# The start of a graph layer: one node tile first, more node tables, and another pace of getting ahead

## The chip, the cores and the metric

The kernel runs on one core of a Trainium2 chip. The metric is the time of one execution on the device, in microseconds; lower is better. The engines named here are TensorE (PE, matrix products; PEld is its weight load), VectorE (DVE), ScalarE (ACT), GpSimd (POOL) and SyncE (SP), which issues most DMAs. Each engine takes its own list of instructions, and semaphores order the lists against each other.

## The reference, cut to what matters

```python
def ssp(x): return softplus(x) - log(2)

h0  = relu(layernorm(x))                                  # x: 12500 nodes x 128
h   = h0 @ W_in2f
Wij = ssp(edge_attr_20 @ W_f1 + b_f1) @ W_f2 + b_f2       # 412500 edges, 20 -> 128 -> 128
Wij = Wij * edge_weight[:, None]
x_ij = h[dst] * Wij                                       # one row of h for each edge
agg = segment_sum(x_ij, src, 12500)                       # summed by the other end
out = x + ssp(agg @ W_o1 + b_o1) @ W_o2 + b_o2
```

The edges are sorted by `dst`, so a run of neighbouring edges needs a few neighbouring rows of `h`. `src` is in no order.

## The kernel before, in words

The edges are cut into 806 chunks of 512 (four tiles of 128). For a chunk the kernel makes an edge value `v` (128 x 512) and a picked node row `hg`, multiplies them into `o` and scatters the rows of `o` by `src` into slot tables in DRAM. Later the slots of a node are loaded back, added and put through the output layer. The steps of a chunk, with the lines of the kernel before:

- `hidden` (L668): two products with `wf1` give `z` for a pair of chunks. `hidden_log` (L675 to L677): ScalarE's Abs, Exp and Ln. `hidden_end` (L684): VectorE makes `r`.
- `value` (L769, L771): four products with `wf2` into the PSUM tile `v` and a fifth, `ones_b` by `bf12_p`, that adds the bias. The bias stands in `bf12_p` as three bfloat16 parts, which `biases` (L306 to L309) and `bias_parts` (L316 to L320) make once.
- `rows` (L621, L623): SyncE reads the chunk's place in the node table from `shifts` and loads 32 rows of the table `h3_t[t]` (`near`). `window` (L760): `at` marks which of these rows an edge wants. `pick` (L780): products of `at` and `near`. `picked` (L789): ScalarE scales by the edge weight into `hg`.
- `columns` (L630 to L658): for 8 groups of 16 tiles, VectorE splits `src` into block and place. `blocks` (L689): `inb`. `rank` and `rank_end` (L708, L741, L713, L733 to L737): two products on the running count `free`, its maximum `top` and the slot number of each edge.
- `message` (L798, L800, L804): VectorE makes `o` from `v` and `hg`; GpSimd issues four indirect DMAs of 128 rows.

The node rows `h` are made by the generator `make_h`, one quad (four tiles of 128 nodes) at a time: load, statistics (L343, L344), a scale `rs` by Ln and Exp on ScalarE (L347, L348), normalisation (L352 to L359), transposes (L364), Relu (L366), product with `win` (L370), and three bfloat16 parts of the result (L372 to L378). It stores them to `h3` and to each small table that holds some of these nodes (L384, L393). A chunk reads from one table alone, `table_of[c]`, so it needn't wait for later quads: table 0 holds the first quad and serves 9 chunks; table q + 1 holds quad q and some tiles on either side. The transposes, the product of `make_h` and the bias product `b12` (L308) all use PSUM tiles of one tag, `acc`, which has one buffer.

The order on every engine is the order in which the program makes the instructions (`tc.manual_schedule()`). A prologue makes constants, the first quad and the first chunk's parts. Then a loop calls `step(k)` for each chunk: message of chunk k, then parts of later chunks, so far ahead as bounds in `step` say. Steps with `k < 10` are not `steady` and their leads grow: the window, the pick and the count (`rank`, up to `k + LR`, LR = 6). After each step the generators in `h` and, later, those of `side` (further quads and the rest of the index work) go on by one yield. DMAs from SyncE and ScalarE share eight semaphores in turn, so that an issue waits until the DMA eight before it has landed.

Of the kernel before, what the change touches and what calls it, by code (L numbers as in the profile page):

```python
# [41 lines left out]
def gnn_kernel(  # L42
# [84 lines left out]


    tables = [(0, QN)]
# [4 lines left out]
    for c in range(NC):  # L134
        n = c * CH * N // n_edges
        table_of.append(0 if n < QN - NEAR - P else min(n // QN, NQ - 1) + 1)
# [46 lines left out]
    def load_x(q):  # L183
        n = min(QT, NTILE - q * QT)
        full = min(n, N // P - q * QT)
        xb = ln.tile([P, QT, P], F32, name="xb")
        if full < n:
            nc.vector.memset(xb[:, full:n, :], 0.0)
            nc.sync.dma_start(xb[:N % P, full, :], x[q * QN + full * P:N, :])
        if full:  # L190
            nc.sync.dma_start(xb[:, :full, :], x[q * QN:q * QN + full * P, :]
                              .rearrange("(c p) f -> p c f", p=P))
        return xb
# [60 lines left out]
    def constants():  # L254

        early[0] = load_x(0)
        part_load(0)
        first_load(0)
        nc.sync.dma_start(win, w_in2f)

        for j in range(NCHUNK):
            nc.sync.dma_start(wf1[32 * j:32 * j + RBF, :], w_f1)

        nc.scalar.preload_act_table_set("natural_log_exp_and_others")
        nc.scalar.dma_start(bf1, b_f1[:, None])
        nc.scalar.dma_start(wf2, w_f2)
        nc.scalar.dma_start(bf2, b_f2[None, :].to_broadcast([P, P]))
        make_identity(nc, ident)
        for _ in bounds(0, nc.gpsimd):
            pass  # L270

        prow_i = early_room[:WP, rows_at + 5 * NC:rows_at + 5 * NC + 1].bitcast(I32)
        nc.gpsimd.iota(prow_i, pattern=[[0, 1]], base=0, channel_multiplier=43)
        nc.gpsimd.iota(places, pattern=[[1, P]], base=0, channel_multiplier=0,
                       allow_small_or_imprecise_dtypes=True)

        nc.gpsimd.memset(after, 1.0)
        nc.gpsimd.affine_select(out=after, in_=after, compare_op=ALU.is_ge, fill=0.0, base=-1,
                                pattern=[[1, P]], channel_multiplier=-1)
        nc.gpsimd.memset(ones_b, 1.0)  # L280
        nc.gpsimd.memset(bf12_p, 0.0)
        nc.gpsimd.memset(zero, 0.0)

        nc.gpsimd.memset(before, 1.0)
        nc.gpsimd.affine_select(out=before, in_=before, compare_op=ALU.is_ge, fill=0.0, base=-1,
                                pattern=[[-1, P]], channel_multiplier=1)
        nc.gpsimd.iota(spare, pattern=[[1, 1]], base=N, channel_multiplier=1,
                       allow_small_or_imprecise_dtypes=True)
        nc.vector.memset(eps, EPS)
        nc.vector.memset(half, 0.5)  # L290
        nc.vector.memset(bad, 0.0)
        nc.vector.memset(rel[:, NPART - 1, :], 0.0)
        nc.vector.memset(ones, 1.0)
        nc.vector.memset(none, 0.0)

        for t in range(QT):
            nc.vector.memset(turn[:, :, t:t + 1], -1.0 if t % 2 else 1.0)
        nc.vector.tensor_scalar(prow_i, prow_i, 7, None, op0=ALU.logical_shift_right)
        nc.vector.tensor_copy(prow, prow_i)
        nc.vector.scalar_tensor_tensor(after, ident, BIG, after, op0=ALU.mult, op1=ALU.add)  # L300

        nc.vector.tensor_scalar(rest_of, after, -1.0, 1.0, op0=ALU.mult, op1=ALU.add)

    def biases(psum):

        nc.vector.tensor_scalar(nbf1, bf1, -1.0, None, op0=ALU.mult)  # L306
        b12 = psum.tile([P, QT, P], F32, name="b12", tag="acc")[:, 0, :]
        nc.tensor.matmul(b12, bf1.to_broadcast([P, P]), wf2, start=True, stop=True)  # L308
        nc.vector.tensor_add(bf12, b12, bf2)  # L309

    def bias_parts():

        left = bf12[:3, :]
        for k in range(3):
            part = ln.tile([3, P], BF16, name="bias_part", bufs=1)
            nc.vector.tensor_copy(part, left)  # L316
            nc.vector.scalar_tensor_tensor(bf12_p[:3, :], part, ident[:3, k:k + 1],
                                           bf12_p[:3, :], op0=ALU.mult, op1=ALU.add)
            if k < 2:
                nc.vector.tensor_sub(left, left, part)  # L320

    def late_loads():
        nc.sync.dma_start(wo1, w_o1)
        nc.sync.dma_start(wo2, w_o2)
        nc.sync.dma_start(bo1, b_o1[:, None])
        nc.sync.dma_start(bo2, b_o2[None, :].to_broadcast([P, P]))

    early = {}
    quads = []


    def make_h(q, psum):

        n = min(QT, NTILE - q * QT)
        xb = early.pop(q, None)
        if xb is None:
            xb = load_x(q)
            for _ in range(3):
                yield
# [39 lines left out]
        for (b, rows), table in zip(tables, h3_t):  # L379
            lo = max(0, b - q * QN) // P  # L380
            hi = min(n, (b + rows - q * QN) // P)
            if lo < hi:
                r = q * QN + lo * P - b
                nc.sync.dma_start(  # L384
                    table[r:r + (hi - lo) * P, :].rearrange("(c p) f -> p c f", p=P),
                    hb[:, lo:hi, :, :].rearrange("p c k f -> p c (k f)"))
                if b + rows == QN:
                    yield
            if q == NQ - 1:
                for r in range(NTILE * P - b, rows, P):  # L390
                    if r >= 0:
                        nc.sync.dma_start(table[r:r + P, :], none)
        nc.sync.dma_start(  # L393
            h3[q * QN:q * QN + n * P, :].rearrange("(c p) f -> p c f", p=P),
            hb[:, :n, :, :].rearrange("p c k f -> p c (k f)"))
        yield
# [136 lines left out]
    with tc.tile_pool(name="edge", bufs=2) as edge, tc.tile_pool(  # L533
# [45 lines left out]

        class Group:  # L580


            def __init__(self, g):
                self.g = g
                self.seg = next(s for s in segs if s.g0 * NCHUNK <= g * NCHUNK < s.c1)
                self.n = min(NCHUNK, NCH - g * NCHUNK)
                if g % NB == 0:
                    f = edge.tile([P, NB, CH], F32, name="f")
                    for j in range(NCHUNK):
                        nc.sync.dma_start(f[32 * j:32 * j + RBF, :, :],  # L590
# [3 lines left out]
                i = g - self.seg.g0  # L594
                if i % SB == 0:
                    w = min(SB, ceil_div(self.seg.c1, NCHUNK) - g) * TG
                    cols = slice(g * TG, g * TG + w)
                    src_i = edge.tile([P, SB * TG], I32, name="src_i")
                    nc.sync.dma_start(src_i[:, :w], src_t[:, cols])
# [5 lines left out]
                if g == 0:  # L605
                    rel_store(0)
                self.rel = edge.tile([WP, NCHUNK, CH], BF16, name="rel", bufs=4)
                nc.sync.dma_start(self.rel, rel_d[g * NCHUNK:(g + 1) * NCHUNK, :][None, :, :]
                                  .to_broadcast([WP, NCHUNK, CH]))
# [16 lines left out]
            def columns(self):  # L626
                if len(self.cols) == 3:
# [9 lines left out]
                    nc.vector.tensor_copy(place[:, :w], src_i[:, :w])  # L637

# [255 lines left out]
        NEXT = table_of.index(1) - 1  # L894
        LG, LW, LR, LZ = 12, 6, 6, 4

# [57 lines left out]
        def step(k, units=()):  # L954
# [6 lines left out]
            steady = k >= 10  # L961
            group((k + LG) // NCHUNK)
            part("rows", min(k + LW, 2 * k + 3, NEXT if k < NEXT - 3 else NCH), rows)
# [19 lines left out]
            if not steady:  # L983
                part("window", k + 1 if k < 1 else k + 2 if k < 6 else k + 3, window)
# [5 lines left out]
            part("pick", k + 1 if k < 8 else k + 2, pick)  # L990
# [10 lines left out]
            upto = max(made["rank"], min(k + LR, k + 1 + (k + 1) // 2))  # L1001
# [81 lines left out]
        def side():  # L1083

            others = rest()
            for i in range(1000):
                if i % 9 == 0 and 2 + i // 9 < NQ:
                    quads.append(make_h(2 + i // 9, psum))
# [3 lines left out]
                if i >= 5 and next(others, 1) and not quads and 2 + i // 9 >= NQ:  # L1092
                    return
                yield

        with tc.manual_schedule():
            constants()
            nc.scalar.activation(count_ps, places, AF.Copy)
            nc.scalar.activation(prow_ps, prow, AF.Copy)
            h = [make_h(q, psum) for q in range(2)]  # L1100
            next(h[0])
            next(h[0])
            relative(0)
            shift(0)
            group(0)
            early[1] = load_x(1)
            next(h[0])
            part("hidden", 0, hidden)
            part("blocks", 0, blocks)
            next(h[0])  # L1110
            ready = ranks(0)
            next(ready)
            next(h[0])
            part("log", 0, hidden_log)
            next(ready, None)
            made["rank"] = 0
            next(h[0])
            part("rows", 1, rows)
            biases(psum)
            part("end", 0, hidden_end)  # L1120
            part("window", 0, window)
            bias_parts()
            group(1)
            aside = side()
            for k in range(-1, max(NCH, max(units) + 1)):
# [9 lines left out]
                for m in h:  # L1135
                    next(m, None)
                if k > NEXT - 3:
# [103 lines left out]
```

## Time and profile before

| | us |
|---|---|
| median of 3 runs | 4251.6 |
| the runs | 4243.63, 4254.37, 4251.6 |
| the profiled execution, its own time | 4236.61 |
| span of its instructions | 4234.9 |
| busy: PE, DVE, ACT, POOL | 3371.9, 3352.9, 2329.8, 3095.9 |
| scatters of GpSimd (L804) | 3224 of 959 ns |

How to read the profile's lines: the groups give line, engine, operation, output <- input, count, then after the bar the busy time, the mean in ns of one, and after the second bar the idle time of the engine just ahead of them with what ended most of it. The timeline gives start and duration in us, the engine, the line and the operation; neighbouring instructions of one kind are merged (x4), and square brackets hold the idle time before and what ended it. SPq and ACTq are the queues from which DMAs are issued. A product of float32 shows as two matmul records. PEclk in a window is the share of TensorE's clock that was granted there.

### The profile page before, as it was taken

The numbers are of one execution on the slowest core, as the hardware profiler recorded it, in microseconds if no ns is written. First come the engines' busy times: TensorE is split into PE (matmuls) and PEld (weight loads), VectorE is DVE, ScalarE is ACT, GpSimd is POOL, SyncE is SP. The second block draws the span as 40 slices with busy tenths as digits, with TensorE's granted clock in tenths as the row PEclk, the third lists the DMA queues.
The fourth block names the chain that finished last, engine by engine and source line by source line (L and its number), as shares of the span: only waits on it lengthen the run. The fifth ranks groups of instructions, "written<-read, shape, count | busy, mean of one in ns | idle before, by whom it ended". The sixth has DMA issues, their size and how long they took to land. (4 is left out here: it accounts for less than half of the span.)

```text
span 4234.9 us, 73728 instructions
## 1 busy us (share of the span) xinstructions
PE 3371.9 (80%) x22378; PEld 2543.6 (60%) x22378; DVE 3352.9 (79%) x6752; ACT 2329.8 (55%) x4686; POOL 3095.9 (73%) x3246
## 2 busy tenths in 40 slices
PE   6766666666666666689998899898898988888888
PEld 4444444444444444467777777777776777767777
DVE  8877766776666656678888888888888998999978
ACT  5665565655555555555555555555555555555535
POOL 5777777777777777777777777777777777777760
PEclk9877877877777777789999999999999999999999
DMA  5765555555444454366787777877787768767667
GB/s 171 213 192 180 176 175 177 157 159 159 126 118 132 121 164 125 107 193 210 229 269 213 216 212 211 267 229 218 214 243 234 229 203 270 234 203 204 184 183 232
DMA packets 515591, 820.92 MB, mean 194 GB/s; under 512 B 177075, under 2 KB 312871, under 8 KB 515187
## 3 DMA queue, kind: packets, MB, share of 16 engines
q1 hardware_dynamic: 411586, 602.85, 49.2%
q0 software_dynamic: 103168, 213.15, 15.3%
q8 instruction: 181, 2.97, 0.3%
q14 instruction: 224, 1.83, 0.1%
q10 hardware_dynamic: 432, 0.13, 0.0%
HBM read 419.09 MB, written 396.64 MB: 193 GB/s over the span
## 5 line engine op out<-in xcount | busy, mean ns | idle before, releaser
L804 POOL DMA_INDIRECT slots<-o,slot x3224 | 3092.5, 959 | 1010.8 <-issue 770.3
L769 PE MATMUL v<-wf,r 128*128 128x128 f32 x6448 | 1066.6, 317 | 540.7 <-DVE o L800 539.1
L769 PEld LDWEIGHTS v<-wf,r 128*128 128x128 f32 x6448 | 924.7, 221 | 590.3 <-DVE o L800 571.2
L789 ACT ACTIVATE hg<-picked,rcut 128x128 f32<-128x128 f32 x3224 | 907.7, 368 | 630.9 <-PE picked L780 292.5
L866 PEld LDWEIGHTS acc<-to,m 128*128 128x128 f32 x8132 | 1017.2, 201 | 235.9 <-issue 142.0
L866 PE MATMUL acc<-to,m 128*128 128x128 f32 x8132 | 1078.8, 289 | 32.5 <-DVE to L853 22.1
L675 ACT ACTIVATE a<-z,bf 128x1024 f32<-128x1024 f32 x403 | 450.4, 1118 | 853.5 <-PE z L668 853.0
L668 PE MATMUL z<-f,wf 20*128 20x512 f32 x1612 | 527.2, 734 | 224.8 <-DVE r L684 223.3
L853 DVE TENSOR_TENSOR to<-count_ps,m 128x512 f32<-128x512 f32 (+3 forms) x824 | 641.8, 804 | 65.6 <-DMA m<-slots 34.7
L800 DVE TENSOR_TENSOR o<-v,hg 128x512 f32<-128x512 f32 x806 | 550.5, 683 | 48.8 <-PE v L771 25.0
L798 DVE COPY o<-place 128x8 f32<-128x8 f32 x403 | 77.0, 191 | 610.6 <-DMA slots<-o,slot 609.9
L760 DVE TENSOR_TENSOR at<-count_ps,rel 96x512 bf16<-96x512 f32 x806 | 545.7, 677 | 0.0
L684 DVE SCALAR_TENSOR_TENSOR r<-z,nbf,a 128x1024 f32<-128x1024 f32 x403 | 513.9, 1275 | 21.1 <-ACT a L677 21.1
L677 ACT ACTIVATE a<-a,half 128x1024 f32<-128x1024 f32 x403 | 462.8, 1148 | 13.1
L713 DVE TENSOR_REDUCE top<-free 128x4 f32<-128x392 f32 x806 | 446.7, 554 | 8.1 <-PE free L708 8.1
L689 DVE TENSOR_TENSOR inb<-count_ps,blk 128x392 f16<-128x392 f32 x806 | 447.4, 556 | 0.0
L676 ACT ACTIVATE a<-a 128x1024 f32<-128x1024 f32 x403 | 426.0, 1057 | 12.8
L780 PEld LDWEIGHTS <-at 96*128 96x128 bf16 x3224 | 256.0, 105 | 251.1 <-DVE at L760 104.0
L668 PEld LDWEIGHTS z<-f,wf 20*128 20x128 f32 x1612 | 138.8, 210 | 409.6 <-DVE r L684 362.2
L780 PE MATMUL picked<-near,at 96*128 96x128 bf16 x3224 | 343.2, 234 | 32.1 <-DVE at L760 26.8
L771 PE MATMUL v<-bf_p,ones_b 128*128 128x512 bf16 x806 | 353.3, 438 | 0.0
L741 PE MATMUL free<-inb,rest_of 128*128 128x392 f16 x806 | 302.9, 376 | 12.6 <-DVE top L713 12.6
(112 smaller groups left out, 1428.2 us busy)
## 6 DMA issues: line engine op xcount, KB each, us to landing
m<-slots SPq DMA_DIRECT2D x311, 387.0 KB
m<-slots SPq DMA_DIRECT2D x317, 258.0 KB
rel<-rel_d SPq DMA_DIRECT2D x202, 384.0 KB
m<-slots SPq DMA_DIRECT2D x172, 322.5 KB
slots<-o,slot POOLq DMA_INDIRECT x3224
slots<-zero SPq DMA_DIRECT2D x96, 387.0 KB
slots<-zero SPq DMA_DIRECT2D x64, 516.0 KB
f<-in_f_t SPq DMA_DIRECT2D x404, 80.0 KB
```

Source lines behind the costliest of these rows:

```text
L668: nc.tensor.matmul(z[:, k, :], wf1[rows, :], self.f[rows, :], start=True, stop=True)
L675: nc.scalar.activation(a, z, AF.Abs, bias=bf1)
L677: nc.scalar.activation(a, a, AF.Ln, bias=half, scale=0.5)
L684: nc.vector.scalar_tensor_tensor(r, z, nbf1, a, op0=ALU.max, op1=ALU.add)
L760: nc.vector.tensor_tensor(at, prow_ps.to_broadcast([WP, CH]), self.rel[:, c, :], op=ALU.is_equal)
L769: nc.tensor.matmul(v[:, i, :], r[:, i * P:(i + 1) * P], wf2, start=i == 0, stop=False, skip_group_check=True)
L780: nc.tensor.matmul(ps[:, i, :], at[:, i * P:(i + 1) * P], near, start=True, stop=True)
L789: nc.scalar.activation(hg[:, i, :], ps[:, i, :], AF.Copy, scale=self.rcut[:, j:j + 1])
L800: nc.vector.tensor_mul(o[:, :, :P], v, hg)
L804: put = nc.gpsimd.indirect_dma_start(out=views[j % VIEWS], out_offset=bass.IndirectOffsetOnAxis(ap=self.slot[:, j:j + 1], axis=0), in_=o[: ...
L853: nc.vector.tensor_tensor(to[:, :n, :], count_ps[:, None, :].to_broadcast([P, n, P]), self.m[u][:, :n, P:].to_broadcast([P, n, P]), op=ALU ...
L866: nc.tensor.matmul(self.acc[b // QT][:, i, :], m[:, j, :P], to[:, j, :], start=t == 0, stop=t == self.seg.tiles(b) - 1)
```

## The change

- `make_h` no longer goes by quads alone: the list `made_h` makes tile 0 alone, then tiles 1 to 3, then quads. A new table of 128 rows is put ahead of the others and serves chunks 0 to 4; the table of the first quad serves chunks up to 22. Which rows may be loaded is asked of `served()`, which follows what has been stored.
- The two generators of the first quad go on together: after a step `h[0]` by one yield, `h[1]` by two, and from step 4 on `h[2]` by one. `side` starts after step 11 instead of after step 5.
- `biases` is a generator of four pieces: the bias product comes first in the prologue, and ScalarE casts the three parts into partitions 0 to 31, 32 to 63 and 64 to 127 of `bf12_p`; `ones_b` is one in partitions 0, 32 and 64 alone.
- Loads are dealt out anew: `win`, two of the four copies of `wf1`, `bf1` and `wf2` on ScalarE's queue; `x` of tiles 1 to 3 and `src` before `f`; `bf2` on SyncE, after the first group's loads.
- Constants, the shift of the table rows and the columns are made later or in two pieces, between the pieces of the first tile.
- The leads grow over 20 steps (`RAMP`) instead of 8 to 10.

```diff
+    made_h = [(0, 1), (1, QT - 1)]
+    made_h += [(t, min(QT, NTILE - t)) for t in range(QT, NTILE, QT)]
-    tables = [(0, QN)]
+    tables = [(0, P), (0, QN)]
...
-        table_of.append(0 if n < QN - NEAR - P else min(n // QN, NQ - 1) + 1)
+        table_of.append(0 if n <= P - 2 * WR else 1 if n < QN - P - WR
+                        else min(n // QN, NQ - 1) + 2)
...
         early[0] = load_x(0)
         part_load(0)
         first_load(0)
-        nc.sync.dma_start(win, w_in2f)
-        for j in range(NCHUNK):
-            nc.sync.dma_start(wf1[32 * j:32 * j + RBF, :], w_f1)
+        early[1] = load_x(1)
         nc.scalar.preload_act_table_set("natural_log_exp_and_others")
+        nc.scalar.dma_start(win, w_in2f)
+        for j in range(2):
+            nc.scalar.dma_start(wf1[32 * j:32 * j + RBF, :], w_f1)
         nc.scalar.dma_start(bf1, b_f1[:, None])
         nc.scalar.dma_start(wf2, w_f2)
-        nc.scalar.dma_start(bf2, b_f2[None, :].to_broadcast([P, P]))
...
     def biases(psum):
-        nc.vector.tensor_scalar(nbf1, bf1, -1.0, None, op0=ALU.mult)
         b12 = psum.tile([P, QT, P], F32, name="b12", tag="acc")[:, 0, :]
         nc.tensor.matmul(b12, bf1.to_broadcast([P, P]), wf2, start=True, stop=True)
+        yield
+        nc.vector.tensor_scalar(nbf1, bf1, -1.0, None, op0=ALU.mult)
         nc.vector.tensor_add(bf12, b12, bf2)
-    def bias_parts():
...
+        nc.scalar.activation(bf12_p, bf12, AF.Copy)
+        yield
+        nc.vector.tensor_sub(bf12, bf12, bf12_p)
+        for r in (slice(P // 4, P // 2), slice(P // 2, P)):
+            nc.scalar.activation(bf12_p[r, :], bf12[r, :], AF.Copy)
+        yield
+        r = slice(P // 2, P)
+        nc.vector.tensor_sub(bf12[r, :], bf12[r, :], bf12_p[r, :])
+        nc.scalar.activation(bf12_p[r, :], bf12[r, :], AF.Copy)
...
-        NEXT = table_of.index(1) - 1
+        def served():
+            for c in range(NCH):
+                start, rows = tables[table_of[c]]
+                if stored[0] < min(NTILE, ceil_div(start + rows, P)):
+                    return c - 1
+            return NCH
+        RAMP = 20
...
-            steady = k >= 10
+            steady = k >= RAMP
-            part("rows", min(k + LW, 2 * k + 3, NEXT if k < NEXT - 3 else NCH), rows)
+            part("rows", min(k + LW, 2 * k + 3, served()), rows)
...
-                part("window", k + 1 if k < 1 else k + 2 if k < 6 else k + 3, window)
+                part("window", k + 1 + max(0, k) * 2 // (RAMP - 2), window)
-            part("pick", k + 1 if k < 8 else k + 2, pick)
+            part("pick", k + 1 if k < RAMP - 2 else k + 2, pick)
-            upto = max(made["rank"], min(k + LR, k + 1 + (k + 1) // 2))
+            upto = max(made["rank"], min(k + LR, k + 1 + (k + 1) * (LR - 1) // RAMP))
...
         with tc.manual_schedule():
             constants()
+            bias = biases(psum)
+            h = [make_h(i, psum) for i in range(3)]
+            next(h[0])
+            window_rows()
             nc.scalar.activation(count_ps, places, AF.Copy)
             nc.scalar.activation(prow_ps, prow, AF.Copy)
+            group(0)
+            nc.sync.dma_start(bf2, b_f2[None, :].to_broadcast([P, P]))
+            columns = groups[0].column_parts()
+            next(h[0])
+            next(bias)
+            relative(0)
+            rel_load(groups[0])
+            next(h[0])
+            more_constants()
+            next(h[0])
+            next(bias)
+            next(h[0])
+            part("hidden", 0, hidden)
...
                 step(k, now)
-                for m in h:
-                    next(m, None)
-                if k > NEXT - 3:
+                next(h[0], None)
+                next(h[1], None)
+                next(h[1], None)
+                if k > 3:
+                    next(h[2], None)
+                if k > 11:
                     next(aside, None)
```

## The prediction

> **What bounds the kernel now.** I read the groups by line first, because the busiest engine need not be the one that sets the end.
>
> ```profile
> span 4234.9 us, 73728 instructions
> ...
> L804 POOL DMA_INDIRECT slots<-o,slot x3224 | 3092.5, 959 | 1010.8 <-issue 770.3
> ```
>
> GpSimd (POOL) is busy for only 73% of the span, but its 3224 scatters take 959 ns each and nearly every one is followed by 0.30 us of issue. Next the timeline of GpSimd alone: does the stream ever stop?
>
> ```profile
> 26.11 1.13 POOL L804 DMA_INDIRECT slots<-o,slot  x1 [21.83 <-DVE o L800]
> ...
> 33.90 0.96 POOL L804 DMA_INDIRECT slots<-o,slot  x1 [2.87 <-DVE o L800]
> ...
> 41.38 0.96 POOL L804 DMA_INDIRECT slots<-o,slot  x1 [2.75 <-DVE o L800]
> ...
> 51.67 0.96 POOL L804 DMA_INDIRECT slots<-o,slot  x1 [0.50 <-DVE o L800]
> ...
> 62.99 0.96 POOL L804 DMA_INDIRECT slots<-o,slot  x1 [1.12 <-DVE o L800]
> ```
>
> These are the first scatters of chunks 0, 1, 2, 4 and 6, and each waited for VectorE's product o. After 62.99 no idle time over 0.31 us remains. The last scatter starts at 4106.56, so a period is (4106.56 - 62.99) / 3199 = 1.264 us, and a chunk of four takes 5.06. The tail behind the last scatter, 128 us, is not edited. So the time is one number plus a constant: how late the stream runs. I write it as the start of a chunk's first scatter less 5.06 per chunk before it. It is 26.1 for chunk 0, 28.8 for chunk 1, 31.3 for chunk 2, 31.4 for chunk 4 and 32.6 for chunk 6, then it stays. Only this lateness can change, and with the first scatter where it is and no stall at all the change would gain 32.6 - 26.1 = 6.5 us. That is 0.15%. A measurement of this kernel tells about 0.3%, 12.7 us, from no change; a gain of that size needs a lateness of 19.9, and before's first scatter alone is later.
>
> Then the timeline of all engines up to that scatter.
>
> ```profile
> 7.49 0.36 SPq L599 DMA_DIRECT2D src_i<-in_src_t  x1
> ...
> 16.31 0.39 SPq L384 DMA_DIRECT2D h<-hb  x1
> ...
> 18.52 1.28 DVE L684 SCALAR_TENSOR_TENSOR r<-z,nbf,a 128x1024 f32<-128x1024 f32 x1 [1.97 <-ACT a L677]
> ...
> 21.04 2.02 PE L769 MATMUL v<-wf,r 128*128 128x128 f32 x8
> ...
> 22.86 0.63 PE L771 MATMUL v<-bf_p,ones_b 128*128 128x512 bf16 x1
> ...
> 23.42 2.08 PE L668 MATMUL z<-f,wf 20*128 20x512 f32 x4
> ...
> 25.13 0.68 DVE L800 TENSOR_TENSOR o<-v,hg 128x512 f32<-128x512 f32 x1
> 25.57 1.11 ACT L675 ACTIVATE a<-z,bf 128x1024 f32<-128x1024 f32 x1 [3.14 <-PE z L668]
> ...
> 28.86 0.28 ACT L347 ACTIVATE rs<-mv,eps 128x4 f32<-128x4 f32 x1
> ```
>
> Two paths meet in o: x to table (store at 16.31) to picked rows, and hidden layer to r (18.52) to v (21.04 to 23.49). The v path ends last, and o starts at 25.13, behind statistics of the second quad. That second quad's scale rs comes from ScalarE only at 28.86, behind the next pair's Abs, Exp and Ln. Before, VectorE needs it after o.
>
> **The change, part by part.**
>
> *The first tile's table.* The transposes of tile 0 use the single PSUM buffer "acc", and the change puts the bias product b12 into it first. They must wait until VectorE has added bf2 to b12, so for bf2's load. That load moves from third on ScalarE's queue (issued at 1.86) to thirteenth on SP. SP holds an issue until the DMA eight before it has landed (waits of SP: 0.9 us for x, 0.5 us for dst), so the first f load goes out at about 5.3, when dst is in. Four f loads (L590, 1.47 in all), two wf1 loads (0.35 each) and rcut (0.43) put bf2 at 7.9. src_i, as large and issued at 7.49, let VectorE go at 10.47, 2.98 later; so bf2 is there at 10.9, and the transposes start at 11.2 instead of 7.75. One tile then costs 0.45 (transpose), 0.29 (Relu), 0.55 (product) and 0.29 (cast), and VectorE's part .28, .22 and four column operations of 0.23 before the last subtraction: the store goes at about 14.5, 1.8 us earlier than 16.31. It carries a quarter of the bytes; the 128 KB store at 9.06 freed its reader 1.74 later, the 384 KB one 2.63 later, so I take the near end, 1.8. The row's load and landing (18.94 to 20.66, 1.72) follow: picked rows at 18.0 to 18.9 instead of 20.66.
>
> *r of chunk 0.* On VectorE, after that store: the shift's six operations (8.95 to 10.21: 1.3), ten column operations (11.27 to 13.39: 2.1), inb 0.5, a bias subtraction 0.2, at 0.6, top and three small ones 1.1. That is 5.8, so r starts at 20.3, not 18.52. Its logarithms end by 18 (z after the tile's product at 12.4, 2.08 + 3.4), hidden. r ends at 21.5; v and bias take 2.45 (21.04 to 23.49): 24.0; z of the next pair ends 4.46 behind v's start (25.50 - 21.04): 26.0. ScalarE's three casts of bias parts (at most 0.29 each) sit in its idle time and are ready by 18; the DVE operations they replace stood at 20.31 to 22.6 beside v. Worth zero either way.
>
> *The added wait.* The loop now advances the second h generator twice per step. So VectorE's order has, ahead of o of chunk 0, the operations that need rs of tiles 1 to 3. rs is queued on ScalarE behind Abs, Exp, Ln of pair 1: 26.0 + 3.4 (25.57 to 28.96) + 0.5 = 29.9. Then three small operations and three scalings (0.2 and 0.28 each), 1.4: o starts at 31.4, ends at 32.0, and the scatter starts 0.30 later: 32.3, against 26.11. Behind that wait stand o, at of chunk 1 and r of pair 1; GpSimd and TensorE wait for them. What the earlier table and the bias casts give is eaten here.
>
> The Trainium skill ("TensorE: Matmul & The Clock Gate", Architectural detail) says that ScalarE and VectorE take their instructions strictly in order; the row at 25.13 agrees, since v was ready at 23.49. If o could pass, the first scatter would come at 25.0.
>
> *Chunk 1.* Before, from at (25.73) to the end of the two free products (29.97) is 4.24, to o 1.06 more (31.88 to 32.94), and o follows at's predecessor by 0.6: 5.95 between scatters, 0.9 over 5.06. Lateness 33.2.
>
> *Chunk 2.* In one step come z 2.08, logarithms 3.4, Relu 0.5, products 1.2, cast 0.5, hg 1.14, cast 0.55, subtraction 0.55, top and slots 1.1, one behind the other through in-order engines, since both halves of the second generator now fall there: 11.0, less the 1.1 by which the free products precede o. That is 10 us at the slow matmul rate, 9 at the fast one (z 1.13 at 43.89). I take 9.3, nearer the fast rows: lateness 37.4, before 31.3.
>
> *Chunks 3 to 20.* Before loses another 1.4 here. In after the leads of counts, windows and picks grow over 20 steps instead of 8 to 10, so less is in hand when TensorE is slow. Price from a row: o of chunk 5 at 55.71 to o of chunk 6 at 62.03 is 6.32, 1.26 over the period, in slow matmuls. The clock column of the windows view shows a mean of 0.83 from 50 to 200 us; at half clock or full that is 35% of the time, 5.6 of 16 chunks: 7.1. The third generator adds VectorE work of some 1.7 in each of two steps where about 1 is free: up to 1.6 more. So 0 to 8.7, and I take 3.8, below the middle, since before's lead of one or two chunks covered more than half of its slow stretches (1.4 lost). Rows for chunks 5 on wait for tiles 1 to 3 in their table; they are issued two steps ahead of use, as chunk 9's were, and I price them at zero, at most 5 us.
>
> The side work starts six steps later, in cover; a 128-row table serves chunk 4, whose first node is near 62 (15.5 nodes a chunk), so no repair pass starts.
>
> **Sum.** 37.4 + 3.8 - 32.6 = 8.6 us later; bounds 4.8 and 13.5. The profiled execution has 4236.6 (span 4234.9): 4245.2. The median of the runs is 15.0 above it, so 4260.2 against 4251.6: 0.2% slower, within what can be told.
>
> The same page (Part 1) says that the clock is halved after an idle window of about 3.4 us. Rows agree in kind: z takes 2.08 at 23.42, 1.13 at 43.89, 2.08 at 54.19. By that rule TensorE, idle here from 26 to 32, is slow again in chunk 1; with the fast rate there, chunks 1 and 2 would cost 1.2 less.
>
> **Rivals.** *Slower than can be missed: slow matmuls through the ramp.* Little is in hand against a slow TensorE before step 18. It decides once more than six of chunks 3 to 18 are slow (4.8 + 6.4 x 1.26 = 12.8); nine give 4251.6 + 4.8 + 11.3 = 4267.7. For: 0.66 at 50 to 60 us. Against: fast rows at 66 to 80. 0.22. *Rows late:* chunk 5's row waits behind four stores on SP; 8.6 + 5 = 13.6, 4265.2. 0.06. *A gain:* the wait on rs is shorter than I think and the slow ramp of leads stops all stalls; with the scatter at 25.0 the lateness falls by 7.6, 4244.0. Against it stands VectorE's order. 0.10, of it 0.04 beyond 0.3% by the spread of runs.
>
> **Numbers.** The forecast has 0.62. Slower 0.22 + 0.06 = 0.28; faster 0.04; within 0.3% 0.62 + 0.06 = 0.68. Bounds 4256 to 4265, the rivals at 4244 and 4268, and the 11 us spread of the runs give 4247 to 4273.
>
> **What would show it.** Right: the first scatter at 31 to 33, preceded on VectorE by a wait for rs of some 6 us; tile 0's transposes at about 11; a gap of 9 us or more between the scatters of chunks 1 and 2; no gap after chunk 20; 1.264 a scatter. Wrong: a first scatter before 28, or stalls after 130 us, or a changed tail.

## The result and the profile after

The changed kernel takes 4261.7 us (median of 13 runs, 4254.5 to 4269.5) against 4249.2 for the kernel before (13 runs beside them): a ratio of 1.0031, 95% interval 1.0023 to 1.0040, so 10 to 17 us slower. The profiled execution of the changed kernel has 4257.6, 21.0 above that of before; the latter lay well below its median, so the medians are the measure and the profile shows the places.

Two lines of the page of the changed kernel, the span and the group of scatters:

```profile
span 4255.9 us, 73743 instructions
...
L830 POOL DMA_INDIRECT slots<-o,slot x3224 | 3094.3, 960 | 1026.8 <-issue 769.9
```

The busy time of the scatters has hardly moved (3092.5 before), their idle time has grown by 16.0. The timeline of GpSimd alone tells where. A stop, here and below, is the idle time in the brackets less the usual 0.30 of issue. These are first scatters of chunks 0 to 4, 8 and 9:

```profile
32.52 1.13 POOL L830 DMA_INDIRECT slots<-o,slot  x1 [27.48 <-DVE o L826]
...
38.45 0.96 POOL L830 DMA_INDIRECT slots<-o,slot  x1 [1.01 <-DVE o L826]
...
49.35 0.96 POOL L830 DMA_INDIRECT slots<-o,slot  x1 [6.16 <-DVE o L826]
...
55.30 0.96 POOL L830 DMA_INDIRECT slots<-o,slot  x1 [1.20 <-DVE o L826]
...
62.35 0.96 POOL L830 DMA_INDIRECT slots<-o,slot  x1 [2.31 <-DVE o L826]
...
88.20 0.96 POOL L830 DMA_INDIRECT slots<-o,slot  x1 [3.95 <-DVE o L826]
...
94.28 0.96 POOL L830 DMA_INDIRECT slots<-o,slot  x1 [1.34 <-DVE o L826]
```

The stream begins 6.4 us later than before (26.11), stops for 5.9 us ahead of chunk 2, and goes on stopping to chunk 12. The lateness, in the prediction's measure (5.056 per chunk, unrounded), is 32.5, 33.4, 39.2, 42.1 (chunk 4), 47.8 (chunk 8) and 49.7 (chunk 20), against 32.7 before at chunk 20. The last scatter starts at 4125.15, 18.6 later than before, and 2.4 more lie behind it: together the 21.0.

Now the timeline of all engines up to the first scatter:

```profile
10.69 0.29 DVE L318 TENSOR_TENSOR bf<-b,bf 128x128 f32<-128x128 f32 x1 [4.22 <-DMA bf<-in_b_f]
...
11.13 0.45 PE L375 MATMUL xps<-ident,xb 128*128 128x128 f32 x1 [3.33 <-DVE bf L318]
...
14.59 0.34 SPq L395 DMA_DIRECT2D h<-hb  x1
...
20.35 1.28 DVE L710 SCALAR_TENSOR_TENSOR r<-z,nbf,a 128x1024 f32<-128x1024 f32 x1
...
21.68 2.08 PE L795 MATMUL v<-wf,r 128*128 128x128 f32 x8 [1.65 <-DVE r L710]
...
24.12 2.08 PE L694 MATMUL z<-f,wf 20*128 20x512 f32 x4
...
29.87 0.20 ACT L359 ACTIVATE rs<-rs 128x3 f32<-128x3 f32 x1
30.11 0.16 DVE L365 TENSOR_TENSOR r<-rs 128x3 f32<-128x3 f32 x1 [6.12 <-ACT rs L359]
...
31.54 0.69 DVE L826 TENSOR_TENSOR o<-v,hg 128x512 f32<-128x512 f32 x1
```

`bf12` waits 4.22 for `bf2`, and tile 0's transposes wait for `bf12`. The edge values are done at 24.2 (the bias product runs from 23.55 for 0.63), but `o` starts at 31.54: VectorE stood 6.12 at the first operation that needs `rs` of tiles 1 to 3.

The same view ahead of chunk 2, the largest stop:

```profile
36.31 2.08 PE L694 MATMUL z<-f,wf 20*128 20x512 f32 x4
...
44.45 0.56 DVE L386 TENSOR_TENSOR left<-hps,hb 128x384 f32<-128x384 f32 x1 [5.21 <-ACT hb L383]
```

VectorE waits 5.21 for the second generator's cast `hb`, which ScalarE makes behind the logarithms of this `z`; the count and `o` of chunk 2 stand behind it.

Last, the same view ahead of chunk 8, the second largest of the stops after the first scatter:

```profile
80.29 2.02 PE L795 MATMUL v<-wf,r 128*128 128x128 f32 x8
...
83.16 0.57 DVE L739 TENSOR_REDUCE top<-free 128x4 f32<-128x392 f32 x1 [2.86 <-PE free L734]
...
84.24 0.28 DVE L354 BATCH_NORM_STATS2 st<-xb 128x6 f32<-128x128 f32 x1
...
85.83 0.53 DVE L739 TENSOR_REDUCE top<-free 128x4 f32<-128x392 f32 x1
...
87.24 0.68 DVE L826 TENSOR_TENSOR o<-v,hg 128x512 f32<-128x512 f32 x1
```

TensorE works at its slow rate (2.02 for `v`; 1.11 where it is fast). VectorE waits 2.86 for the count behind that `v`. Then come the third generator's statistics (84.24 to 85.83, 1.6) and a second count (85.83 to about 87.0, 1.1), all ahead of `o`. In a step without these two, chunk 7, the stop was 0.9; with 2.7 on top it would be 3.6, and 3.95 - 0.30 of issue = 3.65 is what stands there. A second count falls into steps 3, 7 and 11 (and 15 and 19, with no stop behind them), where the bound of `RAMP` goes up by one more: the stops ahead of chunks 4 (2.0), 8 (3.65) and 12 (0.4) are the places. Another 0.4 in chunk 12 is one scatter of 1.37 us; before has such a one too (1.36 at 54.20).

### The profile page after: what moved, and what is told of

Read it like the earlier page. It is cut to its first block, busy times and chain, and to the rows that moved or that the text cites. A ratio compares the mean times of both kernels' runs of the same rounds, so it can differ in the third digit from the quotient of the medians.

```text
span 4255.9 us, 73743 instructions
## 1 busy us (share of the span) xinstructions
PE 3414.8 (80%) x22378; PEld 2565.3 (60%) x22378; DVE 3352.3 (79%) x6752; ACT 2331.0 (55%) x4695; POOL 3098.3 (73%) x3250
## 5 line engine op out<-in xcount | busy, mean ns | idle before, releaser
L795 PE MATMUL v<-wf,r 128*128 128x128 f32 x6448 | 1083.2, 320 | 510.7 <-DVE o L826 507.4
L795 PEld LDWEIGHTS v<-wf,r 128*128 128x128 f32 x6448 | 939.9, 224 | 560.4 <-DVE o L826 539.7
L694 PE MATMUL z<-f,wf 20*128 20x512 f32 x1612 | 544.0, 756 | 214.8 <-DVE r L710 214.0
L739 DVE TENSOR_REDUCE top<-free 128x4 f32<-128x392 f32 x806 | 445.4, 553 | 24.2 <-PE free L734 24.2
L806 PE MATMUL picked<-near,at 96*128 96x128 bf16 x3224 | 346.2, 235 | 41.9 <-DVE at L786 41.9
```

Of the source, the lines that this page charges most:

```text
L694: nc.tensor.matmul(z[:, k, :], wf1[rows, :], self.f[rows, :], start=True, stop=True)
L795: nc.tensor.matmul(v[:, i, :], r[:, i * P:(i + 1) * P], wf2, start=i == 0, stop=False, skip_group_check=True)
L806: nc.tensor.matmul(ps[:, i, :], at[:, i * P:(i + 1) * P], near, start=True, stop=True)
```

## The experiments

They ran in three batches. In that of e5 to e8 the kernel before takes 4253 us. In that of e1 to e4 it takes 5340 and in that of f1 to f4 5259: there the granted clock of the profiles is 0.80 to 0.81 instead of 0.87 to 0.88. The record gives chip number 2 for both the batch at 4253 and that at 5340, and number 8 for that at 5259, so what sets the clock isn't shown. Ratios are always to the kernel before in the same batch. The changed kernel itself wasn't run at the lower clock. "Late" is the lateness at chunk 20 in the profile of that run.

| run | with the wait for rs ahead of o of chunk 0 | leads | clock | first scatter | late | ratio (95%) |
|---|---|---|---|---|---|---|
| before | no | old | 0.88 | 26.1 | 32.7 | 1 |
| after | yes | new | 0.87 | 32.5 | 49.7 | 1.0031 (1.0023 to 1.0040) |
| e5 (after again) | yes | new | 0.87 | 32.1 | 47.4 | 1.0035 (1.0022 to 1.0048) |
| e6 | no | new | 0.87 | 25.2 | 41.9 | 1.0029 (1.0020 to 1.0039) |
| e7 (and bf2 early) | no | old | 0.87 | 22.5 | 32.9 | 0.9996 (0.9987 to 1.0005) |
| e8 (two tiles first) | no | old | 0.88 | 24.2 | 33.2 | 1.0000 (0.9990 to 1.0009) |
| e1 (e6's kernel) | no | new | 0.80 | 25.1 | 57.4 | 0.9995 (0.9979 to 1.0011) |
| e2 | yes | old | 0.80 | 32.0 | 67.5 | 1.0023 (1.0006 to 1.0041) |
| f1 (e2's kernel) | yes | old | 0.81 | 32.1 | 65.2 | 1.0010 (0.9998 to 1.0022) |
| e4 (filler) | yes | new | 0.80 | 32.5 | 66.2 | 1.0027 (1.0012 to 1.0043) |
| e3 (before, new leads) | no | new | 0.80 | 25.9 | 55.0 | 1.0001 (0.9983 to 1.0018) |
| f4 (e3's kernel) | no | new | 0.80 | 26.1 | 58.8 | 0.9996 (0.9982 to 1.0011) |
| f2 | no | old counts, new windows and picks | 0.80 | 25.5 | 58.6 | 1.0012 (0.9998 to 1.0025) |
| f3 | no | old | 0.80 | 24.9 | 55.1 | 0.9998 (0.9984 to 1.0012) |

**The second generator goes on by one yield after step -1 (e1, e6).**

```diff
                 next(h[1], None)
-                next(h[1], None)
+                if k >= 0:
+                    next(h[1], None)
```

> The changed kernel, but the second generator makes only one yield after step -1, so VectorE's operations that need rs of tiles 1 to 3 stand behind o of chunk 0. Theory (the wait on rs): the bias product of chunk 0 ends at 24.2, so o starts there and the first scatter at about 25.2 instead of 32.5; the stream's final lateness falls by some 6, and the kernel is 5 to 8 us slower than before instead of 12.5. Rival (the slower leads): the first scatter is earlier too, but GpSimd loses the same us again at chunks 1 to 14, and the time stays at +11 to +13.

> Once more the changed kernel in which the second h generator goes on by one yield, not two, after step -1, beside the changed kernel on the same chip. Wait theory: first scatter at 25, and the stream 6 us less late than in the changed kernel from chunk 5 on, so 0.14% below it. Rival (short leads alone are the loss): first scatter at 25 as well, but the stream just as late as the changed kernel's by chunk 10, and the same time.

The timeline of GpSimd in e6, first scatters of chunks 0, 1, 2 and 8:

```profile
25.19 1.13 POOL L830 DMA_INDIRECT slots<-o,slot  x1 [20.14 <-DVE o L826]
...
34.25 0.96 POOL L830 DMA_INDIRECT slots<-o,slot  x1 [4.13 <-DVE o L826]
...
42.54 0.96 POOL L830 DMA_INDIRECT slots<-o,slot  x1 [3.53 <-DVE o L826]
...
80.17 0.96 POOL L830 DMA_INDIRECT slots<-o,slot  x1 [4.20 <-DVE o L826]
```

The first scatter comes where the forecast had it, 7 us earlier. Chunks 1 and 2 eat some 0.5 of that, and 5.5 to 7.8 are left at chunk 20 (47.4 and 49.7 against 41.9): up to there the wait is real and is not only moved. But from chunk 2 on the stream loses 9.5 more, as in the changed kernel, and the time is still 1.0029. In lateness at chunk 20 the wait is less than half of the loss. How much of it reaches the end isn't shown: the medians of e5 (5 runs) and e6 (10 runs) lie 3.6 apart, too little for these few runs to tell from nothing, and the profiles are apart by only 2.4 at chunk 800 (54.4 against 52.0). At the lower clock e1 came out at the time of before, but that stream has other stops (below), which can hide the leads' part.

**The changed kernel itself (e5).**

> The changed kernel itself, nothing edited, so that the next three stand beside it on one chip. My theory (the wait for rs ahead of o of chunk 0, then short leads in slow matmuls): first scatter at 32.5, ratio to before 1.002 to 1.004 wherever the scatter stream runs without idle time after the ramp. If the ratio is 1.000 here, the loss is one of the first chip alone.

It gives the ratio again, and the same stops: 5.9 ahead of chunk 2, 1.8 ahead of chunk 4, 3.7 ahead of chunk 8.

**One yield, the leads of before, and bf2 back on ScalarE's queue (e7).**

```diff
         nc.scalar.dma_start(wf2, w_f2)
+        nc.scalar.dma_start(bf2, b_f2[None, :].to_broadcast([P, P]))
...
-        RAMP = 20
+        RAMP = 10
...
-                part("window", k + 1 + max(0, k) * 2 // (RAMP - 2), window)
+                part("window", k + 1 if k < 1 else k + 2 if k < 6 else k + 3, window)
...
-            part("pick", k + 1 if k < RAMP - 2 else k + 2, pick)
+            part("pick", k + 1 if k < 8 else k + 2, pick)
...
-            upto = max(made["rank"], min(k + LR, k + 1 + (k + 1) * (LR - 1) // RAMP))
+            upto = max(made["rank"], min(k + LR, k + 1 + (k + 1) // 2))
...
-            nc.sync.dma_start(bf2, b_f2[None, :].to_broadcast([P, P]))
...
-                next(h[1], None)
+                if k >= 0:
+                    next(h[1], None)
```

> Three parts undone at once: one yield of the second generator after step -1, the leads of before, and bf2 back as the fourth load on ScalarE's queue. What stays of the change: the table of tile 0, the larger table for chunks up to 22, ScalarE's bias casts. Wait and leads theory: first scatter at 23 to 24, transposes of tile 0 at about 8, lateness from chunk 10 on equal to before's within 3 us, so a ratio of 0.999 to 1.001. Rival (making one tile alone, and then three, is itself the loss, since the second generator's work falls among chunks 1 and 2): still 1.002 or more.

All of the loss is gone. The timeline of GpSimd in e7, first scatters of chunks 0, 1, 2 and 8:

```profile
22.46 1.13 POOL L831 DMA_INDIRECT slots<-o,slot  x1 [17.41 <-DVE o L827]
...
31.51 0.96 POOL L831 DMA_INDIRECT slots<-o,slot  x1 [4.13 <-DVE o L827]
...
40.66 0.96 POOL L831 DMA_INDIRECT slots<-o,slot  x1 [4.40 <-DVE o L827]
...
71.87 0.96 POOL L831 DMA_INDIRECT slots<-o,slot  x1 [0.80 <-DVE o L827]
```

The timeline of all engines in e7, the two lines that answer to 10.69 and 11.13 above:

```profile
7.86 0.29 DVE L319 TENSOR_TENSOR bf<-b,bf 128x128 f32<-128x128 f32 x1 [0.39 <-DMA bf<-in_b_f]
...
8.30 0.45 PE L376 MATMUL xps<-ident,xb 128*128 128x128 f32 x1 [0.95 <-DVE bf L319]
```

And the same view of e7 ahead of chunk 8:

```profile
66.00 1.13 PE L796 MATMUL v<-wf,r 128*128 128x128 f32 x8 [0.37 <-DVE o L827]
...
67.72 0.57 DVE L740 TENSOR_REDUCE top<-free 128x4 f32<-128x392 f32 x1 [0.80 <-PE free L735]
...
70.91 0.68 DVE L827 TENSOR_TENSOR o<-v,hg 128x512 f32<-128x512 f32 x1
```

Ahead of chunk 8 stand the same statistics and the same two counts (the second at 70.39), but VectorE waits 0.80 for the first count instead of 2.86, and GpSimd's stop is 0.5 instead of 3.65. This chunk alone doesn't price the leads, for the `v` ahead of that count took 1.13 here and 2.02 in the changed kernel (80.29). But elsewhere `v` is slow in e7 too: 2.02 to 2.05 in chunks 5, 7, 9 and 10 (51.20, 60.93, 71.74 and 77.23), with stops of 0.1, 0, 0.4 and 0 ahead of them. The changed kernel, slow in chunks 5, 7 and 9, stops for 0.7, 0.9 and 1.0 there. So slow products alone need not stop the stream. That they do with less in hand is how I read these rows; no run at this clock changed the leads alone. From chunk 2 on e7 loses 2.4, e6 9.5: the leads, with whatever `bf2` still costs by then, are worth about 7. `bf2` brings 2.8 at the transposes (11.13 to 8.30) and 2.7 at the first scatter (25.2 to 22.5), and 1.9 of it are left at chunk 2.

What e7 also shows is where the purpose of the change ends. Its first scatter is 3.65 earlier than before's. Stops of 3.8 and 4.1 ahead of chunks 1 and 2 take that back: before has 2.6 and 2.4 there.

**Two tiles first (e8).** On top of e7: the first table has 256 rows, the second generator makes two tiles, starts three steps later and goes on by one yield a step; the third starts four steps later.

```diff
-    made_h = [(0, 1), (1, QT - 1)]
+    made_h = [(0, 2), (2, QT - 2)]
...
-    tables = [(0, P), (0, QN)]
+    tables = [(0, 2 * P), (0, QN)]
...
-        table_of.append(0 if n <= P - 2 * WR else 1 if n < QN - P - WR
+        table_of.append(0 if n <= 2 * P - 2 * WR else 1 if n < QN - P - WR
...
-                next(h[1], None)
-                next(h[1], None)
-                if k > 3:
+                if k >= 2:
+                    next(h[1], None)
+                if k > 7:
                     next(h[2], None)
```

> The kernel of the run before this, with the first table of two tiles (256 rows, ten to twelve chunks) instead of one and the second generator making two tiles, one yield a step from step 2 on. Theory: the second generator's operations no longer crowd chunks 1 and 2, the gap beyond the period between their scatters falls from 6 to under 2 us, and the stream is 1 to 4 us less late than before's: ratio 0.999 to 1.000. Rival (the first chunks are bound by the slow matmul rate, not by the generator): the gaps stay and the ratio is that of the run before this.

The timeline of GpSimd, first scatters of chunks 0, 1, 2 and 4:

```profile
24.23 1.13 POOL L831 DMA_INDIRECT slots<-o,slot  x1 [19.17 <-DVE o L827]
...
32.98 0.96 POOL L831 DMA_INDIRECT slots<-o,slot  x1 [3.82 <-DVE o L827]
...
40.47 0.96 POOL L831 DMA_INDIRECT slots<-o,slot  x1 [2.73 <-DVE o L827]
...
53.28 0.96 POOL L831 DMA_INDIRECT slots<-o,slot  x1 [2.81 <-DVE o L827]
```

The stop ahead of chunk 1 stays (3.5), that ahead of chunk 2 falls only from 4.1 to 2.4, and there is one of 2.5 ahead of chunk 4. There VectorE first waits 2.43 for a count (48.94) behind a `v` of 2.03, and then does 1.2 us of the second generator's work ahead of `o`. The time is that of before. My expectation, stops under 2 us and a gain, failed, and its rival, that the stops stay and the ratio is e7's, fits better; nothing tried here beats the kernel before.

**The leads of before alone (e2, f1).** Of e7's diff the four hunks on `RAMP`, `window`, `pick` and `upto`.

> The changed kernel with the leads of before (windows, picks and counts get ahead in 8 to 10 steps). Theory (the wait on rs): first scatter at 32.5 as in the changed kernel, chunk 2 not earlier, at most 2 to 3 us won at chunks 4 to 14, so +9 to +12 us against before. Rival (the slower leads): the 10 us of gaps that the changed kernel shows at chunks 3 to 14 fall to before's 1.4, so +2 to +5.

> The changed kernel with the leads of before alone (RAMP 10, counts, windows and picks as far ahead as before); the second generator keeps its two yields after step -1. In the runs before this the two undone together with bf2 gave the time of before, the yield alone gave back less than half. If the two losses add up: first scatter at 32, the stream 3 to 9 us less late than the changed kernel's by chunk 20, ratio about 1.0015. Rival (the short leads are the whole loss, the wait for rs is absorbed later): ratio 1.000. Rival (the leads help only once the first scatter is early): ratio 1.003 as in the changed kernel.

Both ran at the lower clock. The first scatter stays at 32, since the wait is untouched, and the stop ahead of chunk 2 is 7.7 and 8.1 there. The gaps don't fall to before's: 3.9 to 5.0 ahead of each of chunks 4, 6 and 8. One kernel gives 1.0023 and 1.0010, the second with an interval that reaches 1, and this doesn't tell the three guesses of f1 apart.

**The new leads in the kernel before (e3, f4).** Its conditions for `steady`, `window`, `pick` and `upto` get those of the change, with 20 steps.

> The kernel before with nothing but the new leads (20 steps). Theory (the wait on rs): first scatter at 26.1 as before and little lost, 0 to +2 us against before, inside what can be told. Rival (the slower leads): gaps of 6 us and more at chunks 3 to 14, so +5 to +9.

> The kernel before with the new, slower leads and nothing else of the change. If short leads cost by themselves in slow matmuls: the first scatter stays at 26.1, the stream stops ahead of chunks 4, 8 and 12, and is 4 to 9 us later than before's 32.7 at chunk 20, ratio 1.001 to 1.002. Rival (short leads cost only beside the second and third generators, which the change puts into the same steps): lateness 33 to 35, ratio 1.000.

No loss (1.0001, 0.9996). But the batches at the lower clock can't settle it. A line of e1's page, the group of scatters there:

```profile
L830 POOL DMA_INDIRECT slots<-o,slot x3224 | 3094.4, 960 | 2109.9 <-DVE o L826 1218.9
```

The scatters wait 1219 us for `o`, all along the stream. VectorE's `o` in turn waits 804 us, in 200 places, for something that the profile doesn't name (it writes "remote"); none of the profiles at 0.87 to 0.88 has such a wait. With the old leads VectorE's count has such a wait, of 4.0 to 6.3 us, ahead of chunks 4, 6 and 8 in e2 and f1 and of 6 and 8 in f3. A stream at the lower clock is not bound by GpSimd, so what is lost or saved by chunk 20 isn't all still there at the end. f4 does show the stops that I expected (4.7, 5.2 and 5.5 ahead of chunks 4, 8 and 12), and its stream is 58.8 late at chunk 20; but f3, with old leads, is 55.1 late there.

**Counts alone, and yield with leads (f2, f3).** f2 adds to e6's edit the `upto` line of e7; f3 is e7 with `bf2` left on SyncE.

> One yield of the second generator after step -1, and the counts alone get ahead as before (half a chunk per step); windows and picks keep the 20 steps of the change. With the slow growth of the counts the stream stopped for 3.9 us ahead of chunk 8 and for about 1 us ahead of chunks 4 and 12, where a second count falls into one step. Count theory: the stop ahead of chunk 8 falls under 1.5 us, the stream is about 36 us late at chunk 20 instead of 41.7, and the ratio is 1.001. Rival (windows and picks are what is short, since at, pick and v follow each o): the stops stay, 41 us late, ratio 1.003.

> One yield of the second generator after step -1 and all leads of before; bf2 stays on SyncE behind the first group's loads. Beside the run that also moved bf2 back this gives the price of the bf2 load: by the table's step (transposes of tile 0 at 11.2 instead of 8) the first scatter comes at 25, not 22.5, and the stream is 1 to 3 us later throughout: ratio 1.000 to 1.001. Rival (bf2 costs nothing, since later chunks take the 2.5 us up): the lateness at chunk 20 is that of the other run, 32.7.

In f2 the stop ahead of chunk 8 is 3.0 and others of 2.8 to 3.6 follow ahead of chunks 10, 12, 14 and 16; 1.0012. Against the count theory, the old counts alone don't remove the stops. But that doesn't speak for windows and picks: f3, where these are old as well, stops for 5.4 ahead of chunk 8 and is 55.1 late at chunk 20. f3's first scatter is at 24.9, as the price of `bf2` said (25); what it costs later can't be read there.

**A filler for TensorE (e4).** Products that nobody reads are put in to keep TensorE busy through the first 20 steps; nothing is left out.

```diff
+        def fill(n):
+            for _ in range(n):
+                nc.tensor.matmul(filled, ones_b, spread(ones_b, 2), start=True, stop=True,
+                                 skip_group_check=True)
...
+            if k < 20:
+                fill(28 if k < 0 else 6)
...
             part("hidden", 0, hidden)
+            fill(14)
```

> The changed kernel with bfloat16 products of 128x256 that nobody reads, put where TensorE is idle: 14 after the first hidden products, 28 at the end of step -1, 6 at the end of each step up to 19. They keep TensorE busy and change no other engine's work. If slow matmuls cost the chunks after the first: first scatter 31 to 32.5, v of chunks 1 to 14 at 1.1 instead of 2.0 us, the gaps of GpSimd at chunks 3 to 14 near 2 instead of 10, and 0 to +6 us against before. If the clock is not what costs (or if the products are merely in the way): +12 to +18.

The stop ahead of chunk 2 falls to 3.4, but those ahead of chunks 4 and 8 are 4.1 and 6.2, and the ratio is 1.0027. The condition of the test wasn't met: `v` took 1.11 in chunk 1 but 1.99 to 2.03 in chunks 2 to 6. So whether fast products would save the stops isn't shown; nor is what the filler does to the time, since the changed kernel wasn't run at this clock.

Over both batches at the lower clock the three runs with the wait for `rs` give 1.0023, 1.0010 and 1.0027 and are 65 to 68 late at chunk 20; the five without it give 0.9995 to 1.0012 and are 55 to 59 late. That is the wait again, some 9 us at chunk 20, whatever the leads.

## Why the prediction was right, and which term was too small

- **What bounds the kernel.** Right, with one limit. At the higher clock the lateness at chunk 20 orders the kernels (33, 33, 33, 42, 47, 50) as the ratios do, within their intervals, and from chunk 20 to 800 the profile of the changed kernel adds only 1.6. But the lateness doesn't stay in every execution, as the prediction had it: e5, the same kernel, adds 7.0 (last section).
- **The first tile's table.** Right: `bf2` at 10.7 (10.9 predicted), transposes 11.13 (11.2), store 14.59 (14.5), `r` 20.35 (20.3). e7 shows the cause: with `bf2` early the transposes start at 8.30.
- **The added wait.** Right in place, size and cause: `rs` at 30.1 (29.9), `o` at 31.54 (31.4), first scatter 32.5 and 32.1 (32.3). e6 removes it and the scatter comes at 25.2; the prediction had 25.0 for that.
- **Chunks 1 and 2.** 33.4 and 33.0 (33.2); then 39.2 and 38.8 instead of 37.4. The step of chunk 2 took 10.9, not 9.3: the slow rate held (`z` took 2.08 at 36.31), and the 10 us given for that case was 0.9 short.
- **Chunks 3 to 20.** The term that was mis-sized: 3.8 taken, 10.5 and 8.6 measured, at or over the upper bound of 8.7. Its mechanism was named. Of the 10.5, the second counts that the new bound puts into steps 3 and 7, which were left out, make 1.1 each and the third generator's statistics 1.6; the stops ahead of chunks 3 to 9 without these are 0.4 to 1.0, together 5.8. The row for a slow chunk (1.26) was too dear, but the number of slow chunks was too small: of chunks 3 to 18 `v` is slow in eight (1.97 to 2.05) and partly slow in two (1.66, 1.75), not in 5.6. That number came from the clock column, which reads 1.00 up to 60 us in the changed kernel while `v` takes 2.02. I chose below the middle because before's leads hid most of its slow stretches, although the change shortens just those leads; e7 against e6 prices that at about 7.
- **The sum.** 8.6 was forecast. The lateness at chunk 20 grew by 15 to 17, the medians by 12.5, the ratio by 0.31%: the edge of what I called telling from no change, though these runs do tell it. Some of the agreement is luck. The forecast, 4260.2, stands on a median of 4251.6 from 3 runs, and 13 runs give 4249.2; as a growth, 12.5 lies about midway between the forecast's 8.6 and the 16.1 of the first rival.
- **The clock rule.** The rule of the Trainium skill ("TensorE: Matmul & The Clock Gate", Part 1) on the clock after an idle window can't be decided here: after the 6.68 us that TensorE idles before 32.88 its products are slow, as the rule has it, but z was slow ahead of that wait as well (2.08 at 24.12).
- **The rivals.** Slow products through the ramp came true in the profile in its own terms: more than six slow chunks, and its price for nine, 11.3, against 10.5 measured. That price fits by chance, since 3.8 of the 10.5 are the third generator and the second counts. The median, 4261.7, lies nearer to the forecast than to that rival's 4267.7, but not the growth. Rows late: no stop ahead of chunk 5 beyond the slow loop (0.7). A gain: not even e7, which has none of the losses, is faster than before, so what the early table and the bias casts bring to the start isn't kept.

Open: which of counts, windows and picks makes the 7 us of the leads, how much of that is `bf2`, and whether the new leads alone would cost before anything at the higher clock. The runs for these came out at the lower clock.

## What to carry to other kernels

Where one engine's stream bounds the whole run, an earlier start is worth only what the next few chunks don't take back: follow its lateness chunk by chunk until it is constant. On engines that work in order, look at what a generator's extra yield puts ahead of the first product, and at which semaphore it waits on. What is made ahead is the cover against slow products at the start; making it grow more slowly can cost there what the steady state doesn't show (about 7 us here, if e7 against e6 is read as above).

## What was not expected of the hardware

- The same kernel takes 4253 us in one batch and 5259 to 5340 in others, with granted clocks of 0.87 to 0.88 and 0.79 to 0.81, and the chip number on record is the same for 4253 and 5340. In the profiles of one kernel at both clocks (e6 and e1) the scatters' idle time is 1017.9 and 2109.9 us.
- TensorE stays at its slow rate, 2.02 for `v`, for most of the time to about 90 us in the changed kernel; before, `v` was at 1.13 from 41 us on with a few slow ones between. The windows view gives a granted clock of 1.00 up to 60 us there, while `z` takes 2.08 at 24.12 and 36.31: that column doesn't show this slow rate in the first tens of microseconds.
- Executions differ by more than their stops at the start. From chunk 20 to 800 the lateness grows by 1.6 and 7.0 in two executions of the changed kernel, by 0.1 in before and by 10 in e6, e7 and e8. The scatters of these three are busy for 3103 to 3104 us (963 ns each), those of before and of the two executions of the changed kernel for 3092 to 3094 (959 or 960), and so are those of e1, which is e6's kernel. So 3 or 4 ns a scatter come to some 10 us, nearly what the change costs; what makes them isn't shown. The tail behind the last scatter, which no edit touches, is 128.3 to 133.4 in the six profiles at 0.87 to 0.88.
